# Layer 1 of a four-layer graph network: first operands in ten interleaved pieces, and each part's sums issued one part ahead

## The chip, the cores and the metric

The kernel runs on one core of a Trainium2 chip. The core has five instruction streams that run side by side: TensorE (PE; loads of its stationary operand are listed as PEld), VectorE (DVE), ScalarE (ACT), GpSimd (POOL) and SyncE (SP), which in this kernel issues the plain DMAs. A name with a q (SPq, POOLq) is the sequencer of the engine: it issues DMAs, takes branches and waits. Sixteen DMA engines move the data. The metric is device time in microseconds (us) of one execution; smaller is better.

## The reference

Four graph layers, each followed by a residual sum and a normalization, over 3125 nodes of 128 features and 100000 edges sorted by target. The change is in the second of them, layer 1:

```python
def _L1_gnn_ref(x, edge_index, W1, b1, W2, b2):
    row, col = (edge_index[0], edge_index[1])
    n = x.shape[0]
    msg = x[col]
    summed = jax.ops.segment_sum(msg, row, num_segments=n)
    deg = jax.ops.segment_sum(jnp.ones((row.shape[0],), x.dtype), row, num_segments=n)
    agg = summed / jnp.maximum(deg, 1.0)[:, None]
    h = jax.nn.relu(agg @ W1.T + b1)
    return h @ W2.T + b2
...
x = _layernorm(x + _L1_gnn_ref(x, edge_index, ...), axis=-1)
```

`row` is the source of each edge, so the sum goes over the outgoing edges of a node.

## The kernel before

Nodes stand in NT = 25 tiles of P = 128; NP = 3200 is their padded number. Layer 0 leaves three tables in device memory: `u_tab`, the features of each node times W1 (per node tile 3 x 128 bf16, three terms whose sum is the fp32 value); `c_tab`, the counts of edges as a matrix of target by source node in bf16; and `x1_tab`, the normalized features.

Layer 1 then computes, per part c of CW = 512 source nodes (NCW = 7 parts, six of 512 and one of 128; parts are numbered 0 to 6 here):

- the **sums** (L1138 to L1143): a matmul of `b1` with the row of degrees `degrow` (L1140, fp32, which the trace shows as two) starts the sum in PSUM tile `y_ps`, of which there are two buffers; then 25 x 3 matmuls (L1143) of `u1` (all of `u_tab`, in SBUF) with `cs`, the part's columns of `c_tab`, are added;
- `hT` (L1145, L1146): VectorE adds `sums` (zero here unless a general path ran), ScalarE takes the relu;
- the **dense layers**, per block of 128 nodes: a matmul with W2 into `o_ps` (L1150, one buffer), VectorE divides by the degree and adds `xn` (L1153), the normalization writes `xq` (L757), TensorE transposes it (L739), multiplies it with the weights of layer 2's q, k and v (`wqkv2`, L1158, into `p_ps`), VectorE copies q behind `xq` (L1159), ScalarE copies k and v to `kv` (L1161), and SP stores both (L1162, L1163). `xq` and `kv` have two buffers each.

Operands: `u1` comes in one DMA of 2.46 MB (L1044), in rows of 19.2 KB per partition. Each `cs` comes in one DMA of up to 3.28 MB (L1137), in rows of 25.6 KB; it has two buffers. Both are issued by SP, in SP's order. Between the two stands a branch (L1057, around a general path that isn't taken in this run): every engine loads a flag and jumps over the path's instructions. Behind it in the source, and behind or just ahead of it in the built order, come the small loads: `w2` (issued from the helper at L343), `b1` (L1117), `b2` (through the helper at L761), three loads of `wqkv2` (L1121), `xn` (L1133, 1.64 MB in rows of 512 B), and `degrow`. This last one is made on the way: the degrees `deg1` are transposed on TensorE (L1127) into a PSUM buffer that the transpose of `w2` used before, copied to `dT` (L1129) and sent through a DMA to one partition (L1131).

The source of a part is written in the order sums, then dense layers. The framework's scheduler orders each engine's instructions; each engine then runs its own list strictly in order and waits on semaphores. In the order it built for this kernel TensorE has both bias matmuls of parts 0 and 1, the sums of part 0, and then the sums of part c+1 with the dense blocks of part c among them. DMAs from SP use eight completion semaphores in turn; a DMA waits until the previous one on its semaphore has landed.

Of the kernel before, what the change touches and what calls it, by code (L numbers as in the profile page):

```python
# [10 lines left out]
BF16 = mybir.dt.bfloat16  # L11
# [7 lines left out]
P = 128  # L19
N = 3125  # L20
NT = 25
NP = NT * P
# [29 lines left out]
CW = 512  # L52
NCW = -(-NP // CW)
# [34 lines left out]
def tile_gnn(ctx, tc, a, out):  # L88
    nc = tc.nc
# [446 lines left out]
    c_tab = dram.tile([NCW * P, NT * CW], BF16, name="c_tab")  # L536
# [200 lines left out]
    def transposed(pool, ps, x, name, tag="tp"):  # L737
        tp = ps.tile([P, P], F32, name="tp", tag=tag)
        T.transpose(tp, x, ident)  # L739
        xT = pool.tile([P, P], F32, name=name)  # L740
        A.activation(xT, tp, AF.Copy)  # L741
        return xT

    def layernorm(pool, dst, y, t):
        st = pool.tile([P, 6], F32, name="bn_st")
        V.bn_stats(st, y)
        mv = pool.tile([P, 2], F32, name="bn_mv")
        V.bn_aggr(mv, st)
        sd = pool.tile([P, 1], F32, name="bn_sd")
        V.tensor_scalar(sd, mv[:, 1:2], 1e-5, None, op0=OP.add)  # L750
        A.activation(sd, sd, AF.Sqrt)
        rs = pool.tile([P, 1], F32, name="bn_rs")
        V.reciprocal(rs, sd)
        if t == NT - 1:

            V.tensor_mul(rs, rs, real)
        V.tensor_scalar(dst, y, mv[:, 0:1], rs, op0=OP.subtract, op1=OP.mult)  # L757
# [14 lines left out]
    u_tab = dram.tile([P, NT * 3 * D], BF16, name="u_tab")  # L772
# [3 lines left out]
    with tc.tile_pool(name="l0", bufs=2) as wp, tc.tile_pool(name="l0s", bufs=1) as sp, \  # L776
# [25 lines left out]
        def prologue(t, x):  # L802

            xT = transposed(wp, ps1, x, "xT", "misc")
            pw = ps1.tile([P, D + HC + H], F32, name="pw", tag="misc")
            T.matmul(pw, xT, w0, start=True, stop=True)
            hw = wp.tile([P, D + HC + H], F32, name="hw")
            A.activation(hw, pw, AF.Copy)
            hq = wp.tile([P, 3, D], BF16, name="hq")
            A.activation(hq[:, 0, :], pw[:, :D], AF.Copy)  # L810
            hrest = wp.tile([P, D], F32, name="hrest")
            V.tensor_sub(hrest, pw[:, :D], hq[:, 0, :])
            A.activation(hq[:, 1, :], hrest, AF.Copy)  # L813
            V.tensor_sub(hq[:, 2, :], hrest, hq[:, 1, :])
            return hw, hq
# [123 lines left out]
        ahead = x1st, prologue(0, x1st)  # L939
        for t in range(NT):  # L940
# [8 lines left out]
            for run in runs(t):  # L949
                hss = []  # L950
                for s0, w, mult in run:
                    o = OFF[t] + s0
                    if s0 + w == n and t + 1 < NT:

                        ahead = x_next, prologue(t + 1, x_next)
# [85 lines left out]

    with ExitStack() as ctx1, tc.tile_pool(name="l1", bufs=2) as wp, tc.tile_pool(name="l1s", bufs=1) as sp:
        u1 = sp.tile([P, NT, 3, D], BF16, name="u1")
        nc.sync.dma_start(u1, u_tab.rearrange("p (t k d) -> p t k d", t=NT, k=3))  # L1044

        more = sp.tile([P, 1], F32, name="more")
        V.tensor_reduce(more, crowd, AX.X, OP.max)
# [9 lines left out]
        with tc.If(general > 0):  # L1057

            with tc.tile_pool(name="l1g", bufs=1) as gp, tc.tile_pool(name="l1gp", bufs=1, space=PSUM) as ps:
# [13 lines left out]
                for t in range(NT):  # L1073
# [27 lines left out]
                    for c in range(NCW):  # L1101
                        w = min(CW, NP - c * CW)
# [5 lines left out]
                for c in range(NCW):  # L1108
                    w = min(CW, NP - c * CW)
# [21 lines left out]
        nc.sync.dma_start(degrow, dT)  # L1131
        xn = sp.tile([P, NT, D], F32, name="xn")
        nc.sync.dma_start(xn, x1_tab.rearrange("(t p) d -> p t d", p=P))  # L1133
        for c in range(NCW):
            w = min(CW, NP - c * CW)
            cs = wp.tile([P, NT, CW], BF16, name="cs")
            nc.sync.dma_start(cs[:, :, :w], c_tab[c * P:(c + 1) * P].rearrange("p (t w) -> p t w", w=CW)[:, :, :w])  # L1137
            y_ps = ps1.tile([P, CW], F32, name="y_ps", bufs=2)  # L1138

            T.matmul(y_ps[:, :w], b1, degrow[:, c * CW:c * CW + w], start=True, stop=False)  # L1140
            for t in range(NT):
                for k in range(3):
                    T.matmul(y_ps[:, :w], u1[:, t, k, :], cs[:, t, :w], start=False, stop=(t == NT - 1 and k == 2))  # L1143
            hT = wp.tile([P, CW], F32, name="hT")
            V.tensor_add(hT[:, :w], y_ps[:, :w], sums[:, c * CW:c * CW + w])  # L1145
            A.activation(hT[:, :w], hT[:, :w], AF.Relu)  # L1146
            for i in range(w // P):
                j = c * (CW // P) + i
                o_ps = ps1.tile([P, D], F32, name="o_ps")
                T.matmul(o_ps, hT[:, i * P:(i + 1) * P], w2T, start=True, stop=True)  # L1150
                V.tensor_add(xn[:, j, :], xn[:, j, :], b2)
                y = wp.tile([P, D], F32, name="y")
                V.scalar_tensor_tensor(y, o_ps, rdeg1[:, j:j + 1], xn[:, j, :], op0=OP.mult, op1=OP.add)  # L1153
                xq = wp.tile([P, 2 * D], F32, name="xq")
                layernorm(wp, xq[:, :D], y, j)
                x2T = transposed(wp, ps1, xq[:, :D], "x2T")
                p_ps = ps1.tile([P, 3 * D], F32, name="p_ps", bufs=2)
                T.matmul(p_ps, x2T, wqkv2, start=True, stop=True)  # L1158
                V.tensor_copy(xq[:, D:], p_ps[:, :D])  # L1159
                kv = wp.tile([P, 2 * D], F32, name="kv")  # L1160
                A.activation(kv, p_ps[:, D:], AF.Copy)  # L1161
                nc.sync.dma_start(kv_tab[j * P:(j + 1) * P], kv)  # L1162
                nc.sync.dma_start(xq_tab[j * P:(j + 1) * P], xq)  # L1163
# [236 lines left out]
```

## Time and profile before

| | us |
|---|---|
| median of 5 runs | 4582.21 (4580.41 to 4586.68) |
| profiled execution | 4582.39 |
| its span, first to last instruction | 4580.6 |
| layer 0 and tables, until the last store of `u_tab` | 0 to 2064 |
| layer 1, from the load of `u1` to the last store | 2066.28 to 2241.69 |
| layers 2 and 3 | 2245 to 4580.6 |

The page's engine shares are averages over these stages: PE 2063.6 us (45%), DVE 3012.7 (66%), POOL 2851.5 (62%), ACT 963.0 (21%). Of PE's time 144.24 us lie in the 148 us from 2094 to 2242, which is layer 1 from its first sum on; from 2064 to 2094 PE is busy 4.76 of 30. The page's chain that ended last names GpSimd's gathers of layers 2 and 3 (L102, 13% of the span). Layer 2 begins with gathers of `xq_tab`, which need all stores of layer 1.

Lines of the timeline read: start, duration, engine, line of the kernel, operation, written tile <- read tiles, number of instructions merged, and in brackets the idle time before it and what ended it. The granted clock of TensorE is a share of its full clock. Buffer numbers are left out of names, so `u1` appears as `u`, `w2` as `w`, `wqkv2` as `wqkv`. A wait that is named after one DMA can belong to another on the same semaphore.

### The profile page before, as it was taken

To read this page: it belongs to the slowest core of one execution; us is meant where nothing else is said; L and a number is where in the kernel's file an instruction comes from. 1 tells how busy PE (TensorE), PEld (TensorE's weight loads), DVE (VectorE), ACT (ScalarE), POOL (GpSimd) and SP (SyncE) were. 2 spreads that over 40 slices of the span, in tenths; PEclk is the share of its full clock that TensorE was granted. 3 is DMA by queue.
4 is the path that set the end of the run, shared out by engine and by line. 5 is a ranking of instruction groups with operands and counts; after the bars stand their busy time and mean duration, and the time that the engine had idled before them with its cause. 6 is when DMAs were issued, how large, how long until landed. Compare 5 with 4: busy or idle time off the path is not lost. (4 is left out here: it accounts for less than half of the span.)

```text
span 4580.6 us, 40130 instructions
## 1 busy us (share of the span) xinstructions
PE 2063.6 (45%) x12141; PEld 1321.4 (29%) x12141; DVE 3012.7 (66%) x6898; ACT 963.0 (21%) x2570; POOL 2851.5 (62%) x2897
## 2 busy tenths in 40 slices
PE   6358678877897877987502232233340000000000
PEld 5245455655665554653201111111110000000000
DVE  8648678877897786972246666566663555564656
ACT  0124334433443342431101111111120000000000
POOL 0477557766676564740277767677745777777776
PEclk9778788988898888988755555555555555555555
DMA  2444324433344333435333333344332333333332
GB/s 72 135 118 114 96 78 118 117 109 109 106 130 110 91 106 84 112 90 212 122 105 113 116 116 116 117 121 137 119 99 84 100 104 96 100 99 101 100 101 81
DMA packets 213051, 498.37 MB, mean 109 GB/s; under 512 B 62329, under 2 KB 109100, under 8 KB 208185
## 3 DMA queue, kind: packets, MB, share of 16 engines
q0 software_dynamic: 136448, 397.65, 30.8%
q1 hardware_dynamic: 76344, 97.76, 6.7%
q8 instruction: 102, 1.67, 0.1%
q14 instruction: 157, 1.29, 0.1%
HBM read 424.65 MB, written 70.63 MB: 108 GB/s over the span
## 5 line engine op out<-in xcount | busy, mean ns | idle before, releaser
L102 POOL DMA_INDIRECT hs<-h_tab,srcx x821 | 899.2, 1095 | 550.2 <-issue 347.0
L102 POOL DMA_INDIRECT kv<-kv_tab,pay_sb x821 | 782.7, 953 | 296.7 <-issue 239.7
L102 POOL DMA_INDIRECT kv<-ktv_tab,pay_sb x821 | 778.6, 948 | 281.4 <-issue 243.7
L1345 DVE TENSOR_TENSOR qk<-kv,qp 128x1024 f32<-128x1024 f32 (+4 forms) x114 | 126.7, 1112 | 494.1 <-DMA kv<-ktv_tab,pay_sb 448.5
L728 DVE TENSOR_REDUCE u<-msg 128x128 f32<-128x1024 f32 (+4 forms) x228 | 384.1, 1685 | 0.0
L879 PE MATMUL zps<-oh,zq 128*128 128x512 bf16 x1232 | 363.6, 409 | 33.7 <-DVE oh L870 33.3
L1193 DVE TENSOR_TENSOR qk<-kv,qp 128x1024 f32<-128x1024 f32 (+4 forms) x114 | 126.6, 1110 | 365.2 <-DMA kv<-kv_tab,pay_sb 344.3
L891 PE MATMUL t_ps<-zw,zT 128*128 128x136 f32 x1232 | 213.1, 302 | 116.5 <-DVE hs L892 98.2
L102 POOL DMA_INDIRECT zs<-z_tab,rel x205 | 216.4, 1055 | 64.3 <-issue 55.3
L724 DVE TENSOR_TENSOR msg<-kv,ex 128x1024 f32<-128x1024 f32 (+4 forms) x228 | 249.6, 1107 | 0.0
L623 ACT ACTIVATE c_oha<-c_oha,srclo 128x50 bf16<-128x50 bf16 (+2 forms) x821 | 202.3, 327 | 217.6 <-DVE c_oha L619 213.4
L830 PE MATMUL lg<-yw,low 128*128 128x8 f32 x1642 | 219.7, 260 | 22.8 <-ACT low L828 14.3
L830 PEld LDWEIGHTS lg<-yw,low 128*128 128x128 f32 x1642 | 211.1, 199 | 62.5 <-ACT low L828 48.1
L891 PEld LDWEIGHTS t_ps<-zw,zT 128*128 128x128 f32 x1232 | 185.4, 204 | 148.7 <-DVE hs L892 109.4
L739 PE MATMUL tp<-ident,xk 128*128 128x128 f32 x100 | 43.2, 432 | 388.1 <-DVE xk L1261 383.4
L883 PE MATMUL pre<-zT,zw 128*128 128x512 f32 x308 | 188.0, 695 | 36.0 <-ACT zT L881 35.4
L885 PEld LDWEIGHTS pre<-ident,hs 128*128 128x128 f32 x1232 | 177.7, 210 | 65.7 <-issue 64.6
L828 ACT ACTIVATE low<-pre 128x512 f32<-128x512 f32 (+2 forms) x215 | 123.1, 574 | 303.6 <-PE pre L885 237.5
L734 ACT ACTIVATE qp<-xqb 128x128 f32<-128x128 f32 x50 | 13.9, 280 | 813.7 <-DVE qk L1345 544.9
L885 PE MATMUL pre<-ident,hs 128*128 128x128 f32 x1232 | 183.7, 295 | 0.0
L821 PE MATMUL pre<-identb,hq 128*128 128x512 bf16 (+3 forms) x645 | 181.3, 374 | 1.8 <-ACT hq L813 1.3
L1263 PE MATMUL p_ps<-wqkv,xkT 128*128 128x384 f32 x200 | 158.7, 896 | 46.3 <-ACT xkT L741 46.3
(395 smaller groups left out, 5173.0 us busy)
## 6 DMA issues: line engine op xcount, KB each, us to landing
rb<-rel_tab SPq DMA_DIRECT2D x77, 256.0 KB
c_tab<-c_sb SPq DMA_DIRECT2D x25, 768.0 KB
cs<-c_tab SPq DMA_DIRECT2D x6, 3200.0 KB
hs<-h_tab,srcx POOLq DMA_INDIRECT x821
kv<-kv_tab,pay_sb POOLq DMA_INDIRECT x821
kv<-ktv_tab,pay_sb POOLq DMA_INDIRECT x821
h_tab<-h SPq DMA_DIRECT2D x25, 132.0 KB
zs<-z_tab,rel POOLq DMA_INDIRECT x205
```

The lines of the kernel that those rows point to most:

```text
L102: return G.indirect_dma_start(out=dst, out_offset=None, in_=table, in_offset=indirect(idx), **kw)
L623: A.activation(oha[:, s, 0, :], oha[:, s, 1, :], AF.Copy, scale=srclo[:, o:o + 1])
L724: V.tensor_tensor(msg[:, :n, :].rearrange("p s (h d) -> p s h d", h=heads), val.rearrange("p s (h d) -> p s h d", h=heads), ex.unsqueeze(3 ...
L728: V.tensor_reduce(u, msg[:, :n, :].rearrange("p s d -> p d s"), AX.X, OP.add)
L821: T.matmul(pre[:, :k], hq[:, i, :], identb.unsqueeze(1).to_broadcast([P, k, P]), start=(i == 0), stop=False)
L830: T.matmul(lg_ps[:, s, :], low[:, s, :], yw8, start=True, stop=True)
L879: T.matmul(zps, zq[:, i, 2 * R * k2:2 * R * (k2 + 1)], ohs[i][:, cols], start=(i + k2 == 0), stop=(i == NK - 1 and k2 == 1))
L883: T.matmul(pre[:, :k], zw[:, :D], zT[:, cols], start=False, stop=False)
L885: T.matmul(pre[:, s, :], hs[:, s0 + s, :D], ident, start=False, stop=(s == k - 1))
L891: T.matmul(t_ps[:, s, :], zT[:, (s0 + s) * P:(s0 + s + 1) * P], zw[:, D:], start=True, stop=True)
L1263: T.matmul(p_ps, xkT, wqkv[:, k, :], start=(k == 0), stop=(k == NTY - 1))
L1345: V.tensor_mul(qk[:, :n], kv[:, :n, :D], qp.unsqueeze(1).to_broadcast([P, n, D]))
```

## The change

Two edits, both in layer 1.

```diff
         u1 = sp.tile([P, NT, 3, D], BF16, name="u1")
-        nc.sync.dma_start(u1, u_tab.rearrange("p (t k d) -> p t k d", t=NT, k=3))
+        cs0 = wp.tile([P, NT, CW], BF16, name="cs")
+        for t0 in range(0, NT, 5):
+
+            nc.sync.dma_start(u1[:, t0:t0 + 5], u_tab.rearrange("p (t k d) -> p t k d", t=NT, k=3)[:, t0:t0 + 5])
+            nc.sync.dma_start(cs0[:, t0:t0 + 5], c_tab[:P].rearrange("p (t w) -> p t w", w=CW)[:, t0:t0 + 5])
...
-        for c in range(NCW):
+
+        def part(c):
+
             w = min(CW, NP - c * CW)
-            cs = wp.tile([P, NT, CW], BF16, name="cs")
-            nc.sync.dma_start(cs[:, :, :w], c_tab[c * P:(c + 1) * P].rearrange("p (t w) -> p t w", w=CW)[:, :, :w])
+            cs = cs0 if c == 0 else wp.tile([P, NT, CW], BF16, name="cs")
+            if c:
+                nc.sync.dma_start(cs[:, :, :w], c_tab[c * P:(c + 1) * P].rearrange("p (t w) -> p t w", w=CW)[:, :, :w])
             y_ps = ps1.tile([P, CW], F32, name="y_ps", bufs=2)
 
             T.matmul(y_ps[:, :w], b1, degrow[:, c * CW:c * CW + w], start=True, stop=False)
             for t in range(NT):
                 for k in range(3):
                     T.matmul(y_ps[:, :w], u1[:, t, k, :], cs[:, t, :w], start=False, stop=(t == NT - 1 and k == 2))
+            return y_ps
+
+        ahead = part(0)
+        for c in range(NCW):
+            w = min(CW, NP - c * CW)
+            y_ps = ahead
+            if c + 1 < NCW:
+
+                ahead = part(c + 1)
             hT = wp.tile([P, CW], F32, name="hT")
```

First, `u1` and the first part's `cs` are loaded together ahead of the branch, in five pieces each, in turn: piece t0 holds five of the 25 node tiles, 0.49 MB of `u1` (rows of 3840 B) and 0.66 MB of `cs` (rows of 5120 B). Second, the load and the sums of a part become a function, which is called for part c+1 ahead of the `hT` and dense layers of part c.

In the order built from it, SP issues the ten pieces (the ninth and tenth wait for the first and second to land, by the eight semaphores), then takes the branch, then loads `w2`, `b1`, `b2`, `wqkv2`, `xn`, `degrow` and `cs` of part 1. The three loads of `w2`, `b1` and `b2` stood ahead of the branch in the order before. TensorE has the bias and sums of part 0, those of part 1, and then the sums of part c+2 with the dense blocks of part c among them; the last dense block of part 4 and those of parts 5 and 6 stand behind the last sum. No instruction is added or removed but the nine DMAs.

## The prediction

> **What bounds the kernel now.** I read the stage first, from the instructions in order of time around layer 1. It runs from 2066.28 us (first operand load) to 2241.69 us (last store). Nothing of layer 2 overlaps it: GpSimd's first gather of layer 2 comes at 2245.30, behind the last store, and after it the sequence is again one stream. So what layer 1 gains or loses at its end the kernel gains or loses. Times are microseconds.
>
> The start, in the timeline (start, duration, engine, line, out<-in):
>
> ```profile
> 2066.28 0.32 SPq L1044 DMA_DIRECT2D u<-u_tab  x1
> ...
> 2077.17 0.82 SPq L1133 DMA_DIRECT2D xn<-x_tab  x1
> ...
> 2077.34 0.45 PE L739 MATMUL tp<-ident,w 128*128 128x128 f32 x1 [14.34 <-DMA wqkv<-in_L_gnn_Wk]
> ...
> 2078.91 2.93 SPq L1131 DMA_DIRECT2D degrow<-dT  x1
> 2081.89 0.90 SPq L1137 DMA_DIRECT2D cs<-c_tab  x2
> 2086.12 5.14 DVE L1151 TENSOR_TENSOR xn<-xn,b 128x128 f32<-128x128 f32 x25 [7.24 <-DMA xn<-x_tab]
> ...
> 2086.47 3.78 PE L1140 MATMUL y_ps<-degrow,b 1*128 1x512 f32 x4 [7.90 <-DMA degrow<-dT]
> ...
> 2093.87 2.72 PE L1143 MATMUL y_ps<-cs,u 128*128 128x512 bf16 x6 [3.63 <-DMA cs<-c_tab]
> ```
>
> The reader is to see two chains that end in the sums (L1143): `u1` then `cs`, landed at 2093.87; and w2, its transpose, `dT`, `degrow`, landed at 2086.47, behind `xn` (2086.12) in the same queue. The first is later by 7.40. After a branch every engine waits for code; these are the sequencer's instructions of the branch's line (duration, first and last start), 5.6 apart on SP:
>
> ```profile
> L1057 SPq COMPARE_BRANCH  x1: 55/55/55, 2069.1 to 2069.1; - x1
> ...
> L1057 SPq EVENT_SEMAPHORE  x1: 17/17/17, 2074.7 to 2074.7; - x1
> ```
>
> Then busy time by stretch (PE, weight load, VectorE, ScalarE, GpSimd, granted clock, DMA share, GB/s): `xn`'s rows of 512 B move at 290, `cs` at 410; once the sums run, PE is full (12 matmuls in 2.00).
>
> ```profile
> 2082.00:2084.00 2.00, 0.00 (x0) 0.00 (x0) 0.00 (x0) 0.00 (x0) 0.00 (x0) 0.50 1.06 290
> 2090.00:2092.00 2.00, 0.25 (x1) 0.10 (x1) 1.27 (x7) 0.00 (x0) 0.00 (x0) 0.50 0.95 410
> ...
> 2158.00:2160.00 2.00, 2.00 (x12) 1.20 (x12) 0.74 (x3) 0.52 (x1) 0.00 (x0) 1.00 1.08 320
> ```
>
> Last the tail, from the timeline. PE is done with the sums at 2232.9; what follows is a chain through two buffers of `xq`: a block is written only when the store of the block two before it has landed.
>
> ```profile
> 2224.53 0.48 PE L1140 MATMUL y_ps<-degrow,b 1*128 1x128 f32 x2
> ...
> 2233.15 0.34 DVE L757 TENSOR_SCALAR xq<-y,bn_mv,bn_rs 128x128 f32<-128x128 f32 x1
> ...
> 2235.92 0.32 SPq L1163 DMA_DIRECT2D xq_tab<-xq  x1
> ...
> 2237.98 0.34 DVE L757 TENSOR_SCALAR xq<-y,bn_mv,bn_rs 128x128 f32<-128x128 f32 x1
> ...
> 2241.28 0.32 SPq L1163 DMA_DIRECT2D xq_tab<-xq  x1
> ...
> 2241.69 0.38 SPq L1162 DMA_DIRECT2D kv_tab<-kv  x1
> ```
>
> **Part by part. 1: operands in pieces, `cs` 0 beside `u1`.** Bytes: `u1` 128x25x384x2 = 2.46 MB, `cs` 128x25x512x2 = 3.28 MB, together 5.73 MB in ten DMAs. Their traffic can begin where `u1`'s began, 2067.0. At `cs`'s 410 GB/s it takes 14.0 and drains at F = 2081.0. That rate comes from rows of 25.6 KB; the pieces' rows of 3.8 and 5.1 KB aren't in the trace. Bounds: 443 GB/s (the best two microseconds of `u1`) gives F = 2079.9, `xn`'s 290 gives 2086.8. I take 410, since 3.8 KB is 5 times from `u1`'s 19.2 KB and 7.5 times from 0.5 KB. So the operands, which ended last before (2093.87), are there 11 earlier, and this wait is gone.
>
> What is late next is the other chain, since the change puts it behind those bytes. In the built program's order SP now issues the ten pieces, then takes the branch, then loads w2, b1, b2 (which stood ahead of the branch before). DMAs use eight completion semaphores in turn, so pieces 9 and 10 wait for pieces 1 and 2, and behind them on SP stand the branch and every later load. Piece 2 has landed at 2067.0 + 1.15 MB/410 + 1.6 (`xn`'s traffic ends at 2084.5, it is used at 2086.1) = 2071.4. From the end of an issue to the next beyond the register load took 2066.60 to 2067.97, so the branch comes at about 2071.8 + 1.4 = 2073.2; code 5.6 later, 2078.8. w2, b1, b2 and three wqkv loads at 0.38 each: `xn` is issued at 2081.1 to 2081.4, also not before piece 9 has landed (F - 1.6 + 1.6). `xn` took 8.95 from issue to use (2077.17 to 2086.12), `degrow` 0.35 more: 2090.7. w2's own chain is shorter: landed about F + 2.5, `degrow` issued 1.57 later, 2085.1, and then it stands behind `xn`. Bias of part 0 alone is half of 3.78, 1.89: the sums begin at S = 2092.6, not 2093.87: **-1.3**. Bounds: F at 2079.9 gives -1.6 (SP's issue of `xn` holds then), 290 GB/s gives +4.1; code loading between 4.6 (GpSimd's branch at 2268.5, next event 2273.1, with little traffic) and twice 5.6: -1.7 to +4.3. ScalarE, PE, VectorE and GpSimd take the branch at 2067.2 to 2067.8 as before; the wait of their code for the flood is covered up to 2083.5, when w2 lands.
>
> `cs` 1, issued behind `degrow` at some 2087, costs nothing: a `cs` took 11.98 from issue to use (2081.89 to 2093.87), and sums 0 cover it until 2111; without that cover each microsecond would count. Later parts keep their distance of one part's sums, 16 at least.
>
> The clock: the first 14 sums took 0.427 each at clock 0.50, later ones 0.2135. Before, a gap of 3.6 lay between bias and sums; now they join, so the busy stretch begins 1.9 earlier: 1.9/0.427 x 0.2135 = **-1.0** (bounds 0 and -3.0, all 14).
>
> The Trainium skill's page "DMA: Bandwidth & Descriptors", section "Measured (HBM→SBUF, 128 partitions, SWDGE, issued from GpSimd)", speaks against pieces: transfers want 1 MiB or more, where it states 341 GB/s. The row says 410 for whole loads and nothing for pieces; by the page's figure, an estimate, F would be 2083.8 and S 2094.2 instead of 2092.6. Its page "Runtime: NRT & Kernel Launch", section "Instruction fetch mechanics", has a taken branch fetch its target by DMA; that agrees with the 5.6 above and would let the flood lengthen it, by how much it doesn't say.
>
> **2: sums one part ahead.** The order already had the sums of part c+1 among the dense blocks of part c; now it is sums 0, sums 1, then dense 0 among sums 2, up to dense 4 among sums 6, and dense 5 and 6 bare. No work is added. PE was full, so the middle can't shorten: from S the sums of part 5 end after 19.19 (sums 0, 2093.87 to 2113.06) + 1.05 (bias) + 75 x 0.2135 = 16.01 + 4 x 22.49 (periods between 2134.56 and 2224.53) = 126.2: 2218.8, less the clock's 1.0: 2217.8. Before it was 2224.53: 6.7 earlier, by one part's dense work that is still to do.
>
> The tail pays this back. Before: 8.62 to the third block's `xq` (2233.15), one turn of the two buffers to the last block (2237.98, 4.83), 3.71 to the last store. After: 7.4 to the third block of part 4 (8.62 less 1.4 for `hT`, add and relu, now long done, plus some 0.2 of order on VectorE), then three turns, to blocks 1 and 3 of part 5 and to part 6. A turn is 2.77 + 2.06 = 4.83 at full clock, 3.30 + 2.06 = 5.36 at half (2237.98 to 2241.28), and the clock fell at 2236.5 in such a tail. 7.4 + 14.5 to 16.1 + 3.7 = 25.6 to 27.2, plus 0 to 0.6 where VectorE's copies queue behind a waiting write. Middle 26.7: the end is 2244.5 against 2241.69, **+2.8**. Part by part: start -1.3, clock -1.0, bias 1 in the stream +1.05, dense work out of the stream -5.4, tail +9.5.
>
> The profiled execution took 4582.39 (span 4580.6), 0.18 above the median of the five; with +2.8 it is **4585.2**, by the median 4585.0. Likeliest case's own range: 4580 to 4590.
>
> **Rivals.** (a) Small loads overtake the flood: w2, `xn` and `degrow` don't queue behind pieces. For: the queue spreads over 16 engines. Against: `degrow` landed 0.35 behind `xn`. Then `degrow` lands some 2 after an issue at 2083, S = 2087 and the end -5.6 from the forecast: 4579.6. Faster by over 0.2% would need S near 2080.5, before the operands are in: only with a tail that also hides.
> (b) Code loading is held by the flood until it drains, and takes its quiet 4.6 then: SP resumes at 2085.6 instead of 2078.8, S + 6.8: 4592.0, slower. For: four engines' code came at 2074.0 to 2074.7, just as `u1`'s traffic thinned. Against: ScalarE's came at 2072.4. It decides from 12 of code loading upward.
> (c) The tail isn't bound by the buffers, if stores land sooner than 2.06: at most three turns by 1 each, 4582.
>
> **Chances.** Forecast with (c) 0.66, of which 0.04 end above 4591.4; (a) 0.16, of which 0.04 below 4573; (b) 0.14; operands and tail both better than any row 0.04, faster. 0.2% is 9.2, about what a measurement of this kernel can tell from no change. So faster 0.04 + 0.04 = 0.08, slower 0.04 + 0.14 = 0.18, same 0.74. The range runs from below (a), 4578, to (b), 4592.
>
> **What would show it.** First sums near 2092.6 with `degrow` and not `cs` as what PE waited for; SP's `xn` issue near 2081.4; ten pieces drained by 2081; sums 5 ended near 2217.8; seven blocks left behind the last sum with turns of about 5 each. Wrong if bias starts before 2087, if SP's code takes over 8, or if stores end within 20 of the end of sums 5.

## The result and the profile after

| | before | after |
|---|---|---|
| median | 4585.07 us of 55 runs (4576.22 to 4596.38) | 4591.5 us of 33 runs (4582.72 to 4603.91) |
| ratio, 95% interval | | 1.0014 (1.0009 to 1.0019) |
| profiled execution, its span | 4582.39, 4580.6 | 4588.85, 4587.0 |
| layer 1, first operand load to last store | 175.41 | 179.07 |
| its first sums, after that load | 27.59 | 30.32 |
| `hT` of part 5 begins, after that load | 158.36 | 156.17 |
| from there to the last store | 17.05 | 22.90 |

The kernel became slower by 0.14%, 4.1 to 8.7 us. Layer 1 accounts for 3.66 of it in the profiled pair; layer 1 itself began 3.16 later after an unchanged layer 0 (2069.44 instead of 2066.28), which single executions vary by (2056.27 to 2065.40 in runs 5 to 8 below). Behind the last store both took the same (2338.9 and 2338.5).

The start of layer 1 in the timeline of the changed kernel (start, duration, engine, line, written <- read, count, and in brackets the idle time before and its releaser):

```profile
2069.44 0.32 SPq L1047 DMA_DIRECT2D u<-u_tab  x1
...
2081.84 0.34 SPq L343 DMA_DIRECT2D w<-in_L_gnn_W  x1
2082.22 0.32 SPq L1121 DMA_DIRECT2D b<-in_L_gnn_b  x1
...
2086.30 0.35 SPq L761 DMA_DIRECT2D b<-in_L_gnn_b  x1
...
2088.35 0.82 SPq L1137 DMA_DIRECT2D xn<-x_tab  x1
...
2088.74 0.45 PE L739 MATMUL tp<-ident,w 128*128 128x128 f32 x1 [22.58 <-DMA wqkv<-in_L_gnn_Wq]
...
2090.30 2.44 SPq L1135 DMA_DIRECT2D degrow<-dT  x1
...
2097.40 5.14 DVE L1167 TENSOR_TENSOR xn<-xn,b 128x128 f32<-128x128 f32 x25 [7.12 <-DMA xn<-x_tab]
...
2097.76 2.07 PE L1147 MATMUL y_ps<-degrow,b 1*128 1x512 f32 x2 [7.80 <-DMA degrow<-dT]
...
2099.76 15.43 PE L1150 MATMUL y_ps<-cs,u 128*128 128x512 bf16 x59
```

PE now waits for `degrow`, no longer for `cs`: the sums follow the bias at once. The surprise is on SP, between `b1` (2082.22, 0.32 long) and `b2` (2086.30): 3.76 in which it issues nothing, though the view of waits shows SP no semaphore wait there. The branch ahead of it is as forecast, 5.5 long (the same view as before, by line):

```profile
L1061 SPq COMPARE_BRANCH  x1: 55/55/55, 2076.0 to 2076.0; - x1
L1061 SPq EVENT_SEMAPHORE  x1: 17/17/17, 2081.5 to 2081.5; - x1
```

The traffic by stretch (last column GB/s): the pieces run at full rate until 2084 and have thinned out by 2088. Below it the DMA queues from 2084.0 to 2086.3 (packets, MB, share of 16 engines): among the data one packet of queue 14, which carries instructions. In the 3 us before, 2081 to 2084, there is none.

```profile
2082.00:2084.00 2.00, 0.00 (x0) 0.00 (x0) 0.00 (x0) 0.00 (x0) 0.00 (x0) 0.50 1.03 415
2084.00:2086.00 2.00, 0.00 (x0) 0.00 (x0) 0.00 (x0) 0.00 (x0) 0.00 (x0) 0.50 0.74 284
2086.00:2088.00 2.00, 0.00 (x0) 0.00 (x0) 0.00 (x0) 0.00 (x0) 0.00 (x0) 0.50 0.30 101
```

```profile
q1 hardware_dynamic: 230, 0.60, 67.6%
q14 instruction: 1, 0.01, 0.9%
```

The tail, in the timeline. The turns of the forecast are the steps between these `xq`: 4.95, 4.16 and 4.23, then 2.84 to the last store. Three of the four waited for a store; the one at 2237.28 has no such wait, it follows VectorE's `bn_rs` of 2237.20, which waited for ScalarE.

```profile
2232.33 0.35 DVE L757 TENSOR_SCALAR xq<-y,bn_mv,bn_rs 128x128 f32<-128x128 f32 x1 [0.36 <-DMA xq_tab<-xq]
...
2237.28 0.34 DVE L757 TENSOR_SCALAR xq<-y,bn_mv,bn_rs 128x128 f32<-128x128 f32 x1
...
2241.44 0.35 DVE L757 TENSOR_SCALAR xq<-y,bn_mv,bn_rs 128x128 f32<-128x128 f32 x1 [0.31 <-DMA xq_tab<-xq]
...
2245.67 0.35 DVE L757 TENSOR_SCALAR xq<-y,bn_mv,bn_rs 128x128 f32<-128x128 f32 x1 [0.38 <-DMA xq_tab<-xq]
...
2248.51 0.38 SPq L1178 DMA_DIRECT2D kv_tab<-kv  x1
```

### The profile page after: what moved, and what is told of

The parts are those of the page before. It is cut to its first block, busy times and chain, and to the rows that moved or that the text cites. A ratio compares the mean times of both kernels' runs of the same rounds, so it can differ in the third digit from the quotient of the medians.

```text
span 4587.0 us, 40137 instructions
## 1 busy us (share of the span) xinstructions
PE 2062.9 (45%) x12141; PEld 1323.9 (29%) x12141; DVE 3013.8 (66%) x6898; ACT 962.8 (21%) x2570; POOL 2845.3 (62%) x2897
## 5 line engine op out<-in xcount | busy, mean ns | idle before, releaser
L830 PE MATMUL lg<-yw,low 128*128 128x8 f32 x1642 | 220.9, 261 | 22.5 <-ACT low L828 14.3
L830 PEld LDWEIGHTS lg<-yw,low 128*128 128x128 f32 x1642 | 212.0, 200 | 63.8 <-ACT low L828 49.0
L883 PE MATMUL pre<-zT,zw 128*128 128x512 f32 x308 | 190.7, 704 | 34.9 <-ACT zT L881 34.2
```

What stands on the lines that cost most here:

```text
L830: T.matmul(lg_ps[:, s, :], low[:, s, :], yw8, start=True, stop=True)
L883: T.matmul(pre[:, :k], zw[:, :D], zT[:, cols], start=False, stop=False)
```

## The experiments

Twelve runs on four chips. Where the table above was measured, and on the chip of runs 5 to 8, the kernel before takes some 4580; on the other three 5470 to 5476, with more spread. There layers 0, 2 and 3 are longer, layer 1 hardly: run 3, which only swaps loads of the changed kernel, took 179.78 for layer 1 on such a chip, against 179.07. So I compare layer 1's own times across chips (good to about 1 us: run 12 is run 10 on another chip, and its last store is 0.78 later) and whole times only with the kernel before on the same chip. The stage's difference to the kernel before lies inside the interval of the ratio in all eleven timed runs here; for the changed kernel itself it is 0.5 below it.

All in us after the first operand load of layer 1 (in runs 4, 5, 7, 8 and 10 to 12 that of `w2`):

| kernel | first sums | `hT` 5 | from there | last store | ratio (95%) |
|---|---|---|---|---|---|
| before | 27.59 | 158.36 | 17.05 | 175.41 | |
| after | 30.32 | 156.17 | 22.90 | 179.07 | 1.0014 (1.0009 to 1.0019) |
| 1 pieces alone | 31.15 | 161.28 | 15.91 | 177.19 | 1.0017 (1.0002 to 1.0031) |
| 2 sums ahead alone | 27.40 | 151.05 | 22.88 | 173.93 | 1.0009 (0.9993 to 1.0025) |
| 3 after, `b2` first | 31.07 | 155.74 | 24.04 | 179.78 | not timed |
| 4 after, small loads first | 31.73 | 157.01 | 23.86 | 180.87 | 1.0015 (1.0001 to 1.0029) |
| 5 as 4, `degrow` by ScalarE | 22.27 | 147.10 | 24.03 | 171.13 | 0.9992 (0.9982 to 1.0001) |
| 6 after, four buffers | 31.32 | 155.67 | 22.15 | 177.82 | 1.0008 (0.9998 to 1.0017) |
| 7 as 5, four buffers | 22.03 | 146.51 | 22.13 | 168.64 | 0.9981 (0.9972 to 0.9990) |
| 8 as 7, old order of sums | 21.71 | 151.76 | 17.00 | 168.76 | 0.9988 (0.9979 to 0.9997) |
| 9 after, bias last | 7.83, again 20.30 | 150.46 | 22.88 | 173.34 | 1.0008 (0.9992 to 1.0024) |
| 10 as 7, bias last, `cs` 1 early | 9.31 | 135.98 | 22.50 | 158.48 | 0.9981 (0.9966 to 0.9997) |
| 11 as 10, old order of sums | 9.77 | 152.21 | 17.25 | 169.46 | 0.9983 (0.9969 to 0.9996) |
| 12 run 10 again | 12.01 | 138.18 | 21.08 | 159.26 | 0.9976 (0.9957 to 0.9996) |

### 1 and 2: each part of the change alone

Run 1 is the kernel before with the ten pieces, run 2 the kernel before with `part(c)` and the loop that calls it one part ahead, `u1` in one load.

> Part 1 of the change alone (ten pieces ahead of the branch; sums ordered as before). All times in us after the first operand load of layer 1; before: first sums 27.6, last store 175.4; after: 30.3 and 179.1. Theory (the start costs what the trace of after shows: small loads behind the flood and behind a late branch): first sums at 30.3 +-0.5, end of sums 5 some 131 later, tail 17.2 as before, last store 178.1, kernel +2.7 against before. Rival (the slowdown is the new order of the sums alone, the pieces bring what the operands' earlier landing suggests): first sums at 26 or earlier, last store at 174 or earlier, kernel not slower than before.

> Part 2 alone (sums one part ahead; operands in one load each, as before). Theory (the middle is bound by TensorE and only the tail moves): first sums at 27.6 as before, since cs ends last there; end of sums 5 at 27.6 + 126.2 = 153.8 (before 158.3), then the tail of after, 23.3 instead of 17.2: last store 177.1, kernel +1.7. Rival (part 2 alone makes the whole 6 of the medians): last store at 180 or later. Second rival (the tail is hidden): last store at 175 or earlier.

In layer 1 the pieces alone cost 1.8 (start +3.6, clock and stream -0.6, tail -1.1, at a mean clock of 1.00 in the tail instead of 0.84), and the sums ahead alone save 1.5: `hT` 5 comes 7.3 earlier, the tail takes 5.8 of that back. The whole times tell the first from no change, not the second. Run 1 came near its theory. Run 2 did not: its last store, 173.93, lies where the second rival put it, but the tail is not hidden, it took 22.88 as in the changed kernel. What came sooner is the end of the stream, 151.05 instead of 153.8: the opening biases of parts 0 and 1 both ran in the wait for `cs`, so that the second, 1.05, isn't in the stream, and some 7 sums ran at the half clock instead of 14.

The two parts do not add up to the change: +1.8 and -1.5 make +0.3, and the changed kernel is at +3.7. On top of the pieces (run 1 to the changed kernel) the sums ahead cost 1.9: `hT` 5 comes 5.1 earlier, and the tail is 7.0 longer, both tails at clock 1.00.

Run 2's SP, in the timeline, shows what a start without the pieces looks like:

```profile
2719.39 0.34 SPq L1121 DMA_DIRECT2D wqkv<-in_L_gnn_Wq  x1
2719.77 0.55 SPq L1121 DMA_DIRECT2D wqkv<-in_L_gnn_Wk  x1
2720.37 0.43 SPq L1121 DMA_DIRECT2D wqkv<-in_L_gnn_Wv  x1
...
2721.01 0.82 SPq L1133 DMA_DIRECT2D xn<-x_tab  x1
2722.01 3.58 SPq L1131 DMA_DIRECT2D degrow<-dT  x1
...
2737.35 34.04 PE L1145 MATMUL y_ps<-cs,u 128*128 128x512 bf16 x150 [3.66 <-DMA cs<-c_tab]
```

Once past the branch, SP issues five DMAs one behind the other, and the sums wait for `cs` as in the kernel before. So the start was lost to part 1, the longer tail came with part 2.

### 3: is it `b2`, or a place in SP's stream?

```diff
-        w2T = transposed(sp, ps1, load(sp, a["L1_gnn_W2"], "w2"), "w2T")
+        b2 = row_of(sp, a["L1_gnn_b2"], D, "b2")
         b1 = sp.tile([1, D], F32, name="b1")
...
-        b2 = row_of(sp, a["L1_gnn_b2"], D, "b2")
+        w2T = transposed(sp, ps1, load(sp, a["L1_gnn_W2"], "w2"), "w2T")
```

> The changed kernel with the small loads behind the branch in the order b2, b1, w2 instead of w2, b1, b2. In the trace of after SP stood still 4.1 between b1 and b2. Theory C (SP waits there for its next piece of code, which is fetched through the same busy DMA engines): the stall stays in front of the third load, now w2, 3 to 5 long, and b2 and b1 go out at once. Theory B (the load of b2 itself, a row repeated to 128 partitions, can't be queued behind the flood): the stall moves in front of b2, the first load. Either way the first sums stay near 30.3, because xn comes after all three.

```profile
2726.34 0.34 SPq L761 DMA_DIRECT2D b<-in_L_gnn_b  x1
2726.73 0.32 SPq L1121 DMA_DIRECT2D b<-in_L_gnn_b  x1
...
2730.80 0.35 SPq L343 DMA_DIRECT2D w<-in_L_gnn_W  x1
```

The gap stayed at the third DMA behind the branch (3.75), now `w2`. It belongs to the place, not to the load. Again one instruction packet ran inside it, 1.65 before SP went on; in the changed kernel it was 1.65 as well.

### 4: the small loads ahead of the pieces

```diff
+        w2 = load(sp, a["L1_gnn_W2"], "w2")
...
+        for i, k in enumerate("qkv"):
+            nc.sync.dma_start(wqkv2[:, i * D:(i + 1) * D], a[f"L2_gnn_W{k}"])
         cs0 = wp.tile([P, NT, CW], BF16, name="cs")
```

> The changed kernel with w2, b1, b2 and the three wqkv loads ahead of the pieces. Theory (what sets the first sums is degrow, queued behind xn, queued behind the flood; the stall at b2 makes xn 4 later): the ten pieces start 2.3 later and drain at 18, xn is SP's first load behind the branch and lands at 25 to 26, degrow just behind it, first sums near 28, last store near 176.7, 2.4 less than after. Rival (w2's own late landing sets it, xn is no matter): the transpose of w2 runs at 8 and the first sums follow the pieces, at 20 to 21, last store near 170.

Both figures were missed, on the late side: the first sums by 3.7, the last store by 4.2. In the timeline, its end included:

```profile
2718.75 0.28 DVE L1134 COPY dT<-dT_ps 25x128 f32<-25x128 f32 x1 [1.32 <-PE dT_ps L1132]
...
2728.73 0.82 SPq L1138 DMA_DIRECT2D xn<-x_tab  x1
2733.22 2.73 SPq L1136 DMA_DIRECT2D degrow<-dT  x1
...
2740.56 2.07 PE L1148 MATMUL y_ps<-degrow,b 1*128 1x512 f32 x2 [21.85 <-DMA degrow<-dT]
...
2888.53 0.38 SPq L1179 DMA_DIRECT2D kv_tab<-kv  x1
...
2891.71 0.38 SPq L1179 DMA_DIRECT2D kv_tab<-kv  x1
```

With `w2` early, `dT` is done at 8.2 after the first load, but SP comes to it only at 22.4: the branch was taken at 12.1 (SP waited for a landed piece before it issued the tenth), 5.4 more until it went on, and now the gap, 3.67, stands behind `xn`. Again one packet of instructions lies in it, 1.74 before its end. The operands were in; one row of 12.5 KB held up the first of 525 matmuls. Layer 1 ends 1.8 later than in the changed kernel: 1.4 at the start and 1.0 in the tail (mean clock 0.89 instead of 1.00), less 0.6 in between. The 177.7 that the next expectation gives for this run is the last store but one (2888.53); the last is at 180.87.

### 5: `degrow` in another engine's queue

```diff
-        nc.sync.dma_start(degrow, dT)
+        nc.scalar.dma_start(degrow, dT)
```

> As the run with the small loads first (last store of layer 1 issued 177.7 after its first load, first sums at 31.7, `degrow` ready to be moved at 8.2 but issued by SyncE at 22.4, behind its branch, `xn` and a standstill of 3.7), with one line changed: `degrow` is moved by ScalarE's queue. Theory (the first sums wait for `degrow`, and that waits for SyncE's instruction stream, not for the operands): `degrow` issued 8 to 9 after the first load, first sums at 13 to 17, last store at 162 to 166, ratio 0.997 to 0.998. Rival 1 (the flood of pieces itself delays whatever is moved): first sums above 22, last store above 169. Rival 2 (the gain at the start is given back, since the sums of part 1 wait for their `cs`, issued behind SyncE's standstill): first sums at 13 to 17, but the sums of part 1 not before 40 and the last store above 169.

```profile
2068.82 0.28 DVE L1134 COPY dT<-dT_ps 25x128 f32<-25x128 f32 x1 [1.23 <-PE dT_ps L1132]
...
2074.64 1.31 ACTq L1136 DMA_DIRECT2D degrow<-dT  x1
...
2081.26 2.07 PE L1148 MATMUL y_ps<-degrow,b 1*128 1x512 f32 x2 [12.48 <-DMA degrow<-dT]
```

Out of SP's list it left 8.7 earlier and the sums began 9.5 earlier, so the chain through `degrow` is what the start hangs on. The stage kept all of it: the last store comes 9.7 earlier than in run 4. The theory's sizes were missed, though, and the numbers lie where rival 1 had them (first sums above 22, last store above 169): ScalarE issued `degrow` 5.5 after `dT` was done, where the expectation had it within 1. The view of that line shows an event of ScalarE's sequencer just ahead of the issue:

```profile
L1136 ACTq EVENT_SEMAPHORE  x1: 17/17/17, 2074.6 to 2074.6; - x1
```

By the trace's semaphore updates it waits for the completion semaphore of the second piece of `cs`, issued 4.9 after the first load; that piece's last update comes at 13.57, and `degrow` is issued at 13.65. ScalarE's DMA takes its turn in the same eight semaphores as SP's. So it is in all six runs with ScalarE's queue (issue 12.6 to 14.7, each 0.07 to 0.08 behind that piece). Rival 1 is thus half right: the pieces held `degrow` up, by its turn and not by a slow transfer, for from issue to use it took 6.6.

### 6, 7 and 8: buffers in the tail, and the old order with a short start

Run 6 is the changed kernel, run 7 is run 5, both with four buffers; run 8 is run 7 with the loop of the kernel before.

```diff
-                xq = wp.tile([P, 2 * D], F32, name="xq")
+                xq = wp.tile([P, 2 * D], F32, name="xq", bufs=4)
...
-                kv = wp.tile([P, 2 * D], F32, name="kv")
+                kv = wp.tile([P, 2 * D], F32, name="kv", bufs=4)
```

> The changed kernel with four buffers instead of two for `xq` and `kv`. Theory (in the tail each turn of two blocks waits for the store of the pair before it, as its third and later `xq` do): the tail from the end of sums 5 to the last store is 18 to 20.5 instead of 23.3, last store at 174.5 to 176.5 after the first load, and start and middle as in the changed kernel (first sums 30 to 31.5). Rival (the turns are set by the chain of VectorE, TensorE and ScalarE through one block): tail 22 to 23.5, last store 178 to 179.5.

> The changed order of sums with the small loads first, `degrow` on ScalarE's queue and four buffers for `xq` and `kv`. If both theories hold, first sums at 13 to 17, tail 18 to 20.5, last store at 158 to 163, ratio 0.9965 to 0.9975. If the start theory fails: first sums above 22. If only the tail theory fails: last store as in the run without the buffers, 162 to 166.

> The same, but with the order of sums of the kernel before (the dense layers of a part stand in the stream behind its own sums). It tells whether part 2 of the change is worth anything once the start is short. Theory (part 2 takes 5 to 7 us out of the stream and gives as much back in the tail, of which four buffers save some): first sums at 13 to 17, last store 1 to 4 us later than with the changed order. Rival (with four buffers the tail of the old order shrinks as well, and the orders are equal): within 1 us of it.

Run 6: the tail went from 22.90 to 22.15, not to 18 to 20.5; the last store, 177.82, is next to the rival's 178. No `xq` of it waits for a store any more; in its place the timeline has this gap:

```profile
2228.48 0.38 SPq L1178 DMA_DIRECT2D kv_tab<-kv  x1
...
2229.09 0.29 DVE L1161 TENSOR_TENSOR hT<-y_ps,sums 128x128 f32<-128x128 f32 x1 [1.05 <-PE y_ps L1150]
...
2231.18 0.35 DVE L757 TENSOR_SCALAR xq<-y,bn_mv,bn_rs 128x128 f32<-128x128 f32 x1
...
2234.94 0.33 SPq L1178 DMA_DIRECT2D kv_tab<-kv  x1
```

The four blocks of part 4 leave in 1.4 steps; then part 5's begin from an empty chain, and its first store follows the last of part 4 by 6.46. The stores were not the only bound: without them the tail is nearly as long, by the chain of engines through a block. The clock hides some of the gain: its mean in the tail was 0.92 in run 6, 1.00 in the changed kernel. At 1.00 in both, run 12 with four buffers has a tail of 21.08, run 9 with two 22.88, so the buffers are worth 1.8. In run 7 they brought 1.9 of tail against run 5 (clock 0.92 and 0.88). Run 7 missed what was expected of it as run 5 did (first sums 22.03, last store 168.64), by the same turn in the semaphores; run 8 came out as its rival said. Both runs 7 and 8 beat the kernel before, and end layer 1 alike: the changed order has its sums done 5.3 earlier and a tail 5.1 longer.

### 9: the bias behind the sums

```diff
-            T.matmul(y_ps[:, :w], b1, degrow[:, c * CW:c * CW + w], start=True, stop=False)
...
-                    T.matmul(y_ps[:, :w], u1[:, t, k, :], cs[:, t, :w], start=False, stop=(t == NT - 1 and k == 2))
+                    T.matmul(y_ps[:, :w], u1[:, t, k, :], cs[:, t, :w], start=(t == 0 and k == 0), stop=False)
+            T.matmul(y_ps[:, :w], b1, degrow[:, c * CW:c * CW + w], start=False, stop=True)
```

> The changed kernel with one edit: in each part the product of `degrow` and the bias closes the group of sums instead of opening it. Theory (in the changed kernel nothing but `degrow`, issued 20.9 and landed 28.3 after the first load, holds up the first sums; their operands lie ready from 18.7): the first sums follow the two transposes that wait for `w2`, which was used at 19.3 there, so first sums at 19.5 to 22 instead of 30.3, and the last store at 168 to 172 instead of 179.1, ratio 0.998 to 0.9995. Rival (the operands or the moved `cs` of part 1, issued behind `xn` and `degrow`, hold the sums up just as long): first sums 19.5 to 22 but the sums of part 1 wait for `cs`, last store above 174, ratio at or above 1.000; or first sums still at 28 or later.

```profile
2716.03 2.72 PE L1149 MATMUL y_ps<-cs,u 128*128 128x512 bf16 x6 [11.10 <-DMA cs<-c_tab]
2727.44 1.06 PE L1149 MATMUL y_ps<-cs,u 128*128 128x512 bf16 x2
...
2728.50 16.29 PE L1149 MATMUL y_ps<-cs,u 128*128 128x512 bf16 x67
...
2747.36 0.49 PE L1166 MATMUL o_ps<-w2T,hT 128*128 128x128 f32 x2 [1.52 <-ACT hT L1162]
...
2752.63 3.65 PE L1149 MATMUL y_ps<-cs,u 128*128 128x512 bf16 x9
```

First sums at 7.83, when the first pieces were in; then PE stood until `w2` was there, whose transpose its list has behind the sixth sum, and the stream ran from 20.30, 10.0 earlier than in the changed kernel. So the operands did not hold it up. The stage kept 5.7 of the 10: in this kernel the scheduler put dense layers of part 0 ahead of the sums of part 1, so that these began only at 44.4, though sums and bias of part 0 had ended at 37.6. With a last store at 173.3 both expectations missed, it lies between them.

### 10, 11 and 12: all of it together

Run 10 is run 7 with the bias last and this; run 11 the same with the old loop; run 12 is run 10 once more.

```diff
+        cs1 = wp.tile([P, NT, CW], BF16, name="cs")
+        nc.sync.dma_start(cs1, c_tab[P:2 * P].rearrange("p (t w) -> p t w", w=CW))
         xn = sp.tile([P, NT, D], F32, name="xn")
```

> Small loads first, `degrow` on ScalarE's queue, the bias last in each group, the `cs` of part 1 issued ahead of `xn`, four buffers for `xq` and `kv`, the changed order of sums. Theory (the start is then bound by the pieces themselves and by `w2` on TensorE): first sums at 8 to 11 after the first load (22.0 in the run with the bias first), end of sums 5 at 133 to 138, last store at 155 to 160, ratio 0.9955 to 0.997. Rival (the pieces land so slowly, the last near 18 to 20, and the `cs` of part 1 near 28 to 33, that TensorE starves): first sums 8 to 11, but the last store above 163.

> The same with the order of sums of the kernel before. In the pair with the bias first the two orders ended alike (last store 168.6 and 168.8): the changed order ended its sums 5 earlier by 5.3 and had a tail longer by 5.1. Theory (part 2 only moves work from the stream to the tail): last store within 1.5 us of the changed order. Rival (with the short start the changed order hides the wait of the first dense layers for `xn`, which lands near 32): the changed order ends 3 us or more ahead.

> The kernel of the run with the bias last, the small loads first and the `cs` of part 1 ahead of `xn`, taken once more for a narrower interval: there its layer 1 ended 16.9 us earlier than in the kernel before (last store 158.5 instead of 175.4), and the medians gave 0.9981 with an interval from 0.9966 to 0.9997. If the stage is what moves the time: ratio 0.996 to 0.9975 where the kernel before takes 4580, last store again at 157 to 160. Rival (the stage gives its gain back later): ratio above 0.9985 with the same last store.

Run 10 in the timeline, and then the one line of run 11 that parts them:

```profile
2730.31 0.59 PE L1152 MATMUL y_ps<-cs,u 128*128 128x512 bf16 x1 [2.02 <-DMA cs<-c_tab]
...
2750.55 16.35 PE L1152 MATMUL y_ps<-cs,u 128*128 128x512 bf16 x75 [0.73 <-DMA cs<-c_tab]
2755.93 3.12 DVE L1170 TENSOR_TENSOR xn<-xn,b 128x128 f32<-128x128 f32 x15 [24.50 <-DMA xn<-x_tab]
```

```profile
2740.14 0.79 PE L1158 MATMUL o_ps<-w2T,hT 128*128 128x128 f32 x2 [6.45 <-ACT hT L1154]
```

PE has work from 9.3 on and loses 0.73 to `cs` of part 1. `xn` lands at 34.9, and only then comes `hT` 0, which stands behind the sums with `xn` in VectorE's list; but TensorE is busy with part 1 meanwhile. In the old order it stands 6.45 for that `hT`. Layer 1 ends 16.9 earlier than before in run 10, 16.2 in run 12, 5.9 in run 11. So here part 2 of the change is worth 11.0 in layer 1, against 1.5 alone, 0.1 in runs 7 and 8 and a loss of 1.9 between run 1 and the changed kernel. Of the 11.0 the wait for `hT` is 6.45, and the wait for `cs` of part 1 is 1.3 longer in run 11 (1.99); the rest is not taken apart, but TensorE's mean clock was 0.77 around that wait. By the whole times runs 10, 11 and 12 are faster than the kernel before (0.9981, 0.9983 and 0.9976). Run 10's ratio is above the range expected of it, run 12's just above (0.9976 for 0.996 to 0.9975), with intervals too wide to tell 0.9985 from 0.9970; that range was meant for a kernel before of 4580, and of 5470 the 16.2 are a smaller share. The two orders are not told apart by the whole times.

## Why the prediction held, and where it did not

The forecast was +2.8, within 0.2%. Layer 1 grew by 3.66 in the profile and the kernel by 4.1 to 8.7 by the ratio: within 0.2% as well, but with an interval wholly above 1, so a small slowdown can be told. The time itself, 4591.5, lies at the upper edge of the stated 4578 to 4592, also because the kernel before took 4585.07 here and 4582.21 in the five executions on which the forecast stands. That the sum came near is luck in part: two terms were mis-sized in opposite directions.

- **The operands' wait is gone: right.** PE waits for `degrow`, not for `cs`. The pieces moved at 404 GB/s on average from 2072 to 2084, near the 410 taken. They were not drained at 14.7 after the first load, but thinned out between 14.6 and 18.6. (With the slower rate of 341, the sum's own rule gives S = 2095.0, not the 2094.2 written there.)
- **SP's branch and its code: right.** Branch at 6.6 (forecast 6.9), 5.45 of code loading (5.6), SP on its way at 12.1 (12.5).
- **"w2, b1, b2 and three wqkv loads at 0.38 each": the step that failed.** SP stood still once more, 3.76, at the third of them. `xn` was issued at 18.9 instead of 15.1, and from there all went as forecast: 9.05 to its use (8.95), `degrow` 0.36 behind it (0.35), bias, sums at 30.3 instead of 26.3. The start term is +2.7 instead of -1.3. That the gap is bound to a place in SP's stream and not to a load is shown by runs 3 and 4; that it lies in the chain that sets the start, by runs 5 and 9.
- **What the gap is.** It stood 2.8 to 4.1 long in every profile with pieces (the changed kernel's and eleven runs'), in each behind the fifth instruction that SP's record has after the branch, be that one or two DMAs; in the two without pieces SP's longest gap there was 0.92 (before, ahead of `degrow`, which waits for `dT`), and 0.03 behind that fifth instruction. It is no turn of a semaphore: where the next instruction waits for one, its last update is 6 us or more older than the gap's end. Nor does it look like a full DMA queue: in run 4 the gap ends with a semaphore event, 0.08 ahead of the next DMA. In all twelve an instruction packet starts in it, the last one 1.6 to 1.7 before SP goes on. So SP waiting for its next instructions is what the traces point to. Not settled is how much of it is the traffic and how much where the code now lies: the change has eight DMAs more (ten pieces for two loads; not nine, as the section on the change has it), and they move that too. No run fills the queues without adding instructions.
- **Rival (b)**, code loading held by the flood, was thus given too little: it named the branch as the place, where nothing was held, and the hold came five instructions later. Its price there, +6.8, is above the 4.0 found. Its condition, that the flood drains first, is not what ended the gap: in run 4 the queues moved 328 GB/s during it.
- **Middle: right; clock: smaller.** From first sums to `hT` 5 it took 125.85, forecast 126.2 - 1.0. Some 12 sums ran at the half clock instead of 14, which is -0.4. That the joined start brought even this is not shown: with the same joined start run 1 had some 7 such sums, and run 2, with the old gap of 3.66, had some 7 as well.
- **The tail: mechanism half right, size too large.** Forecast 26.7 from the end of sums 5, found 22.90 from `hT` 5; before 17.05, so +5.9 instead of +9.5. Blocks did wait for stores, but the three turns took 13.3 instead of 14.5 to 16.1: the last two were 2.43 from `xq` to its store and 1.73 to 1.80 until the buffer was free, where I had 2.77 and 2.06, with PE at its full clock (1.00 through the tail, against 0.84 before), and the last step was 2.8 instead of 3.7. The 2.06 was a misreading. In the kernel before no `xq` of the tail waits for a store in the profile; the one at 2237.98 stands behind a copy of VectorE's that waited 1.61 for TensorE, at the half clock by then:

```profile
2237.77 0.29 DVE L1159 COPY xq<-p_ps 128x128 f32<-128x128 f32 x1 [1.61 <-PE p_ps L1158]
```

- That stores free their buffers sooner is rival (c), which the forecast held possible. The buffers explain little of the tail: without their waits the chain through the engines binds nearly as late, 1.8 sooner at the same clock (runs 9 and 12).
- Start and tail together: forecast +8.2, found +8.6. The sum came out for the wrong reasons in both.

## What to carry to other kernels

When a wait ends last, look up what ended second and whether the change puts it behind the very bytes that it hurries: here a row of 12.5 KB, made from degrees and needed by an opening bias, took the place of 5.7 MB. Another engine's queue is no way past those bytes as long as its DMAs take their turn in the same semaphores: run 5's `degrow` waited for a piece to land. Such an operand is better used last in an accumulation than hurried: the bias behind the sums, the small loads ahead of the pieces, the next part's operand ahead of what is needed later and four buffers in the tail together brought 17 us of layer 1, where the change alone lost 4. And what issuing ahead is worth depends on the rest: from a loss of 1.9 us to a gain of 11 for the same edit, most where it covers a wait that others had hidden until then.

## What the runs showed of the hardware

- An issuing engine can stand still twice behind a taken branch: SP stood 5.1 to 6.5 at the branch, and, in the twelve profiles with pieces, 2.8 to 4.1 again one or two DMAs later, while loads moved (240 GB/s on average in run 3's gap, 328 in run 4's). No semaphore wait shows the second; only the gap between issues and the instruction packets in it do.
- Ten loads of 0.49 and 0.66 MB queued back to back moved at 404 GB/s on average over 12 us and at up to 415 over 2, about as fast as a whole `cs` (410).
- `degrow`, 12.5 KB, took 6.6 from issue to use through ScalarE's queue with pieces still under way (run 5), and behind `xn` on SP's 7.5 in the changed kernel and 7.6 before. No run has it on idle queues.
- The time differs from chip to chip: the kernel before took some 4580 where the table above was measured and on the chip of runs 5 to 8, and some 5470 on three others; each was visited once, so chip and moment are not told apart. Layer 0 and the layers behind layer 1 grew (in run 2 the first load of layer 1 is at 2710 instead of 2066, and 2594 instead of 2339 lie behind it), while a gather of layer 2 took as long (952 and 953 ns). What grew, in the lines compared, is idle time: TensorE's weight loads of one line (L830) waited 94 for ScalarE instead of 48.
